# Two graph layers on one core: the first pair of block rows loaded ahead of x, and row scales spread by two DMAs instead of a matrix product

## The chip, the cores and the metric

The kernel runs on one core of one Trainium2 chip. The metric is the device time of one execution in microseconds, lower is better. Every time below comes from three timed runs of the kernel before the change, or from one profiled execution of it.

## The reference

```python
# x: 4096 x 512, adj: 4096 x 4096 (mostly zeros, none negative), W: 512 x 512, all float32
def _L0(cur, inc_m):
    head = (inc_m > 0).astype(float32)
    head = head / maximum(sqrt(sum(head * head, axis=-1)), 1e-12)
    inc = inc_m + head
    return (inc @ cur) / sum(inc, axis=-1)

def _L1(X, A, W):
    A2 = A + eye(4096)
    d = diagonal(A2) ** -0.5
    temp = A2 @ X @ W.T
    return relu((d[:, None] * A2 * d[None, :]) @ temp)

x = layernorm(x + _L0(x, adj))
x = layernorm(x + _L1(x, adj, W))
```

The part that the change touches is `head`: each row of `adj` gets 1/sqrt(number of its positive entries) added to every positive entry. That number per row is counted before the row can be multiplied, and its inverse root is called the row's scale here.

## The kernel before

All large products are float32 and use a Winograd form of Strassen's scheme: seven products of quarter matrices instead of eight, with sums of quarters as operands. The work has two stages.

**First stage (layer 0, and the sums for layer 1).** A *pair* is two blocks of 128 rows of `adj`, rows j and j + 16 in blocks; there are 16 pairs (`NP`). A pair is cut into four *chunks* (`NC`) of four quarters by 512 columns each, 1 MB, laid out by the host in `adj_q` with the row on the free axis (so that the chunk can be the left operand). Chunk n = 4j + c goes through these steps:

- `load_chunk` (L280) on SP's queue into a ring of three tiles `a`.
- `prepare1` (L373), all on VectorE: L383 adds two raw quarters into `sr` (kept for layer 1 and written to DRAM by POOL at L403, into `oa`); L393 makes a mask, (a > 0) times the scale, for one half, and L395 adds it to `a`, for each half; `add_up` (L156 to L162) makes the four sums `s`. `sr` and the two masks are three tiles of one ring of three (`half_tile`, tag `u`).
- `multiply1` (L405): 4 x 7 products on TensorE (L417; each float32 product stands as two records in the profile) into seven PSUM banks that add up over the four chunks.

When a pair is through, `combine` (L419) takes the seven banks out on ScalarE and VectorE, `layer0` (L445) normalises, `operands` (L458) makes the sums of the next stage's right operands and writes them to DRAM (`ob`). The right operands of this first stage are made from x: `load_x` (L285) brings two blocks of x into a slot, and `build` (L295), four VectorE instructions through `outer_sums` (L121), makes four sums in it. There are 16 slots, all kept.

The scales: `count` (L339) lets ScalarE take the sign of tiles of 128 rows by 512 columns of `adj` in natural order (`nat`, five tiles, loaded by SP), with a running sum per row: 16 tiles give a pair's counts, one per row, with the row on the partition axis. `prepare1` wants the scale along the free axis and on all partitions. So `spread` (L351) turns it: a reduction (L355), `to_scale` (L304 to L308, two VectorE instructions and a square root on ScalarE), a reciprocal (L360), a diagonal matrix times the two scales (L363), a product with a matrix of ones on TensorE (L368) into the spare bank, and a copy to `sc` by ScalarE (L370). For the first pair `count_first` (L310) takes the signs of its four chunks and sums them with products by a matrix of ones (L320), which gives the counts on all partitions at once. The fourth chunk is loaded once for this into the tile `last` and again later for its products.

The order is written out by hand: each engine runs its instructions in the order in which the code issues them, and SP's and POOL's queues do likewise. Before the loop SP loads x for slots 0 to 3, three chunks, the fourth chunk, and the rest of x mixed with natural tiles. In the loop, chunk n + 1 is prepared ahead of the products of chunk n, and the first pair's later slots are built in its rounds c = 0, 1, 2. A pair's spread begins at c = 2 of the pair before (c = 3 for the first).

**Second stage (layer 1).** Two passes of products over all of `adj` (`multiply2`, L243, products at L252), the projection by W (L625), and the last normalisation. The change does not touch it.

Of the kernel before, what the change touches and what calls it, by code (L numbers as in the profile page):

```python
# [8 lines left out]
F32 = mybir.dt.float32  # L9
BF16 = mybir.dt.bfloat16  # L10
# [16 lines left out]
def tile_adj_resnorm_d2(  # L27
# [67 lines left out]
    def spare():  # L95
        return bank(7)
# [8 lines left out]
    nc.gpsimd.memset(eps_t, LN_EPS)  # L105
    tiny = const.tile([P, 1], F32, name="tiny")
    nc.gpsimd.memset(tiny, -(2.0 ** -63))
    dscale = const.tile([P, NB], F32, name="dscale")
    nc.gpsimd.dma_start(out=dscale, in_=diag)

# [10 lines left out]
    def outer_sums(t, b11, b12, b21, b22):  # L121

        nc.vector.tensor_sub(t[:, 0, :], b11, b12)
        nc.vector.tensor_sub(t[:, 2, :], b22, b12)
        nc.vector.scalar_tensor_tensor(t[:, 1, :], t[:, 0, :], -1.0, b22, op0=ALU.mult, op1=ALU.subtract)
        nc.vector.tensor_add(t[:, 3, :], b21, t[:, 1, :])

# [139 lines left out]
    w1_pool = scope.enter_context(tc.tile_pool(name="w1", bufs=2))  # L267
    pools["turn"], pools["work"] = [ring] * 2, work

    ones_f = w1_pool.tile([P, P], F32, name="ones_f", bufs=1)  # L270
    nc.gpsimd.memset(ones_f, 1.0)
    ones_b = w1_pool.tile([P, P], BF16, name="ones_b", bufs=1)
    nc.gpsimd.memset(ones_b, 1.0)
    chunks, sums, slots, counts, scale, natural = {}, {}, {}, {}, {}, {}
    xr = {}

    def half_tile(dtype=F32, width=CW):
        return w1_pool.tile([P, 2, width], dtype, tag="u", name="u", bufs=3)

    def load_chunk(n):  # L280
        a = ring.tile([P, 4, CW], F32, tag="a", name="a")
# [2 lines left out]

    def load_x(kk):  # L285

        s = feats_pool.tile([P, 7, W], F32, name=f"b{kk}")
        lo, hi = x[kk * P:(kk + 1) * P, :], x[(kk + NP) * P:(kk + NP + 1) * P, :]
        nc.sync.dma_start(out=s[:, B11:T4 + 1:T4, 0:H], in_=split(lo))
        nc.sync.dma_start(out=s[:, B21:B22 + 1, 0:H], in_=split(hi))  # L290
        nc.gpsimd.memset(s[:, B11:B21 + 1, H:W], 1.0)
        nc.gpsimd.memset(s[:, T1, H:W], 1.0)
        slots[kk] = s

    def build(kk):  # L295

        s = slots[kk]
        outer_sums(s[:, T1:T4 + 1, 0:H], s[:, B11, 0:H], s[:, T4, 0:H], s[:, B21, 0:H], s[:, B22, 0:H])

    def signs(y, a, accum=None):  # L300

        nc.scalar.activation(y, a, AF.Sign, bias=tiny, scale=2.0 ** 64, accum_out=accum)  # L302

    def to_scale(n, total):  # L304

        nc.vector.tensor_scalar(n, total, 0.5, N / 2, op0=ALU.mult, op1=ALU.add)
        nc.vector.tensor_scalar(n, n, EPS * EPS, None, op0=ALU.max)
        nc.scalar.activation(n, n, AF.Sqrt)  # L308

    def count_first(parts):  # L310

        ps = spare()[:, 0:2 * P].rearrange("p (h i) -> p h i", h=2)
        for c, a in enumerate(parts):
            m = half_tile(BF16, 2 * CW)
            m = m.rearrange("p h (q i) -> p (h q) i", q=2)
            signs(m, a)
            for i in range(CK):
                for z in range(2):
                    first, last = c + i + z == 0, c == NC - 1 and i == CK - 1 and z == 1
                    nc.tensor.matmul(ps, ones_b, m[:, z::2, i * P:(i + 1) * P], start=first, stop=last)  # L320
        s = w1_pool.tile([P, 2, P], F32, name="sc")
        to_scale(s, ps)
        nc.vector.reciprocal(s, s)
        scale[0] = s

    tiles = iter([(j, h, t) for j in range(1, NP) for h in range(2) for t in range(NT)])
    waiting = []
# [18 lines left out]
            signs(nat, nat, counts[j][:, h, t:t + 1])  # L346
            load_natural()

    spreading = {}

    def spread(j, part):  # L351

        if part == 0:
            n = small.tile([P, 2], F32, name="n")
            nc.vector.tensor_reduce(n, counts.pop(j), axis=mybir.AxisListType.X, op=ALU.add)  # L355
            to_scale(n, n)
            spreading[j] = n
        elif part == 1:
            n = spreading.pop(j)
            nc.vector.reciprocal(n, n)  # L360
            d = w1_pool.tile([P, 2, P], F32, name="d", bufs=1)
            for h in range(2):
                nc.vector.tensor_scalar(d[:, h, :], ident, n[:, h:h + 1], None, op0=ALU.mult)  # L363
            spreading[j] = d
        else:
            d = spreading.pop(j)
            ps = spare()
            nc.tensor.matmul(ps[:, 0:2 * P], ones_f, d.rearrange("p h i -> p (h i)"), start=True, stop=True)  # L368
            s = w1_pool.tile([P, 2, P], F32, name="sc")
            nc.scalar.copy(s.rearrange("p h i -> p (h i)"), ps[:, 0:2 * P])  # L370
            scale[j] = s

    def prepare1(n, pieces=1):  # L373


        j, c = divmod(n, NC)
        a, s = chunks[n], scale[j]
        sr, *masks = (half_tile() for _ in range(3))
        sums[n] = work.tile([P, 4, CW], F32, tag="s", name="s")
        for i in range(pieces):  # L380
            w = CW // pieces
            cols = slice(i * w, (i + 1) * w)
            nc.vector.tensor_add(sr[:, :, cols], a[:, A11:A22 + 1, cols],  # L383
                                 a[:, A21, cols].unsqueeze(1).to_broadcast([P, 2, w]))
            for h in range(2):
                t = masks[h]
                y, z = t[:, :, cols], a[:, 2 * h:2 * h + 2, cols]
                if pieces == 1:
                    parts = [[v.rearrange("p q (b i) -> p (q b) i", i=P) for v in (y, z)]]
                else:  # L390
                    parts = [[v[:, q, :].rearrange("p (b i) -> p b i", i=P) for v in (y, z)] for q in range(2)]
                for m, v in parts:
                    nc.vector.scalar_tensor_tensor(m, v, 0.0, s[:, h, :].unsqueeze(1).to_broadcast(list(v.shape)),  # L393
                                                   op0=ALU.is_gt, op1=ALU.mult)
                nc.vector.tensor_add(a[:, 2 * h:2 * h + 2, cols], a[:, 2 * h:2 * h + 2, cols], t[:, :, cols])  # L395
            add_up(sums[n][:, :, cols], a[:, :, cols])
# [6 lines left out]
        nc.gpsimd.dma_start(out=dst, in_=sr.rearrange("p m (k i) -> p (m k) i", i=P))  # L403

    def multiply1(n, acc):  # L405
        c = n % NC
# [58 lines left out]
        nc.gpsimd.dma_start(out=in_outer(2, j, slice(T1, T4 + 1)), in_=t)  # L465


    for kk in range(CK):
        load_x(kk)
    for n in range(3):  # L470
        load_chunk(n)
    last = work.tile([P, 4, CW], F32, tag="s", name="s")
    nc.sync.dma_start(out=last, in_=adj_q[0, NC - 1])
    for kk in range(CK, NP):
        load_x(kk)
        if kk >= 2 * CK and len(waiting) < 5:
            load_natural()
    for kk in range(CK):
        build(kk)
    count_first([chunks[0], chunks[1], chunks[2], last])  # L480
    prepare1(0, pieces=CK)

    C = None
    for n in range(NP * NC):
        j, c = divmod(n, NC)
        if c == 0:
            if j > 0:
                C = combine(acc)
            acc = [bank(m) for m in range(7)]
        if n + 2 >= NP * NC:  # L490
            load_up_to(n + 2 - NP * NC)
        elif n > 0:
            load_chunk(n + 2)
        if j == 0 and c < NC - 1:
            for kk in range((c + 1) * CK, (c + 2) * CK):
                build(kk)
        if j + 1 < NP and c == (3 if j == 0 else 2):
            spread(j + 1, 0)
            if j == 0:
                spread(1, 1)  # L500
                spread(1, 2)
        if n + 1 < NP * NC:
            prepare1(n + 1)
        else:
            prepare(0)
        if 0 < j < NP - 1 and c == 2:
            spread(j + 1, 1)
        multiply1(n, acc)
        if 0 < j < NP - 1 and c == 2:
            spread(j + 1, 2)  # L510
        count(((5, 5, 6, 4) if j == 0 else (6, 6, 0, 4))[c])
        if j == 1 and c == 1:
# [300 lines left out]
```

## Time and profile before

| what | value |
|---|---|
| median of three runs | 2345.42 us (2344.67 to 2349.24) |
| profiled execution | 2345.41 us |
| its span, first to last instruction | 2343.6 us |
| mean granted TensorE clock | 0.990 |
| busy: TensorE, VectorE, ScalarE, POOL | 2277.4, 1832.7, 351.5, 220.7 us |
| end of the first stage's products | 834.55 us |

PE is the TensorE row for products and PEld for loading the left operand, which overlaps it. DVE is VectorE, ACT ScalarE, POOL GpSimd, and SP the engine whose queue issues most loads. In rows of the form "line engine operation out<-in", tile names are those of the program without their numbers. In brackets stands how long the engine was idle before the instruction and what ended that; if several things were waited for, only the last by the profile is named. In a row of windows the columns are the stretch, its length, busy time with number of instructions for PE, PEld, DVE, ACT and POOL, the granted TensorE clock, the busy share of the DMA engines, and GB/s.

### The profile page before, as it was taken

The page shows a single profiled execution, that of the slowest core. Times are in us where ns is not written, and L with a number is a line of the kernel's source. Part 1 is how long each engine was busy: PE and PEld are TensorE (multiplying, and loading weights), DVE is VectorE, ACT ScalarE, POOL GpSimd, SP SyncE. Part 2 cuts the span into 40 slices and gives each one's busy share as a digit, 9 for nine tenths or more (in the row PEclk, how much of TensorE's full clock was granted, in tenths as well). Part 3 has the DMA queues.
Part 4 walks back from the last instruction along what each step waited for, and adds up shares of the span by engine and source line. Part 5 has one row for each costly group of instructions (what it writes and reads, how often), then busy time and mean ns, then how long its engine had stood idle before and what let it go on. Part 6 is the DMA issues. An engine that isn't in the chain of part 4 may idle for free.

```text
span 2343.6 us, 21028 instructions
## 1 busy us (share of the span) xinstructions
PE 2277.4 (97%) x7166; PEld 1352.6 (58%) x7166; DVE 1832.7 (78%) x2727; ACT 351.5 (15%) x806; POOL 220.7 (9%) x372
## 2 busy tenths in 40 slices
PE   4999999999999999999999999999999999999996
PEld 3788888888888844444444444444444444444443
DVE  6898888888889857888666779766567798767796
ACT  3232333323333000000000000000000011200013
POOL 0011111111111110000001100011100000000010
PEclk8999999999999999999999999999999999999998
DMA  9577777777776466575566757567666576765672
GB/s 318 197 252 252 262 244 253 258 255 260 251 256 235 172 261 242 207 276 204 202 252 229 274 186 267 186 237 286 225 238 223 214 253 237 267 231 216 224 260 77
DMA packets 148011, 552.97 MB, mean 236 GB/s; under 512 B 15920, under 2 KB 24128, under 8 KB 108864
## 3 DMA queue, kind: packets, MB, share of 16 engines
q1 hardware_dynamic: 114192, 418.42, 51.0%
q0 software_dynamic: 33712, 133.21, 14.9%
q8 instruction: 57, 0.93, 0.2%
q14 instruction: 50, 0.41, 0.0%
HBM read 438.32 MB, written 113.25 MB: 235 GB/s over the span
## 4 chain that ended last, share of the span: by engine, by line
PE 86%; DVE 8%; issue 3%; DMA 2%; ACT 0%; POOL 0%; SPq 0%; ACTq 0%; DVEq 0%; POOLq 0%
PE q L252 55%; PE q L417 26%; PE q L625 5%; DVE a L395 1%; DVE u L393 1%; DVE s L159 1%; DMA a<-oa 1%; DVE u L383 1%; DMA s<-adj_q 1%; DVE s L161 1%; PE q L645 1%; DMA oa<-u 0%; DVE c L553 0%; DVE s L162 0%; PE q L368 0%
## 5 line engine op out<-in xcount | busy, mean ns | idle before, releaser
L252 PE MATMUL q<-s,ts 128*128 128x512 f32 x1344 | 616.0, 594 | 1.0 <-DVE u L544 1.0
L417 PE MATMUL q<-b,s 128*128 128x256 f32 (+1 forms) x2048 | 488.5, 381 | 2.3 <-DVE s L161 2.3
L159 DVE TENSOR_TENSOR s<-a 128x1024 f32<-128x1024 f32 (+1 forms) x243 | 294.1, 1210 | 203.5 <-PE q L252 173.8
L252 PEld LDWEIGHTS q<-s,ts 128*128 128x128 f32 x1344 | 256.2, 191 | 325.7 <-issue 296.6
L417 PEld LDWEIGHTS q<-b,s 128*128 128x128 f32 x2048 | 389.8, 190 | 61.0 <-DVE s L161 3.7
L417 PE MATMUL q<-b,a 128*128 128x258 f32 (+1 forms) x1536 | 381.8, 383 | 10.1 <-issue 10.1
L252 PE MATMUL q<-a,tr 128*128 128x512 f32 x704 | 333.5, 596 | 5.1 <-DMA tr<-ob 4.2
L417 PEld LDWEIGHTS q<-b,a 128*128 128x128 f32 x1536 | 293.9, 192 | 52.9 <-issue 10.7
L252 PE MATMUL q<-s,tr 128*128 128x512 f32 x448 | 228.8, 592 | 0.0
L252 PEld LDWEIGHTS q<-a,tr 128*128 128x128 f32 x704 | 132.1, 191 | 162.1 <-issue 158.1
L302 ACT ACTIVATE nat<-nat,tiny 128x512 f32<-128x512 f32 x240 | 171.0, 715 | 208.2 <-DMA nat<-adj 208.1
L252 PE MATMUL q<-a,ts 128*128 128x512 f32 x352 | 180.2, 593 | 3.1 <-DVE c L549 2.9
L393 DVE SCALAR_TENSOR_TENSOR u<-a,sc 128x1024 f32<-128x1024 f32 (+1 forms) x142 | 157.6, 1114 | 24.8 <-ACT sc L370 14.4
L161 DVE TENSOR_TENSOR s<-a,s 128x512 f32<-128x512 f32 (+1 forms) x243 | 166.5, 685 | 8.3
L162 DVE TENSOR_TENSOR s<-a,s 128x512 f32<-128x512 f32 (+1 forms) x243 | 166.5, 685 | 8.3
L395 DVE TENSOR_TENSOR a<-a,u 128x1024 f32<-128x1024 f32 (+1 forms) x134 | 157.7, 1177 | 6.8
L252 PEld LDWEIGHTS q<-s,tr 128*128 128x128 f32 x448 | 85.1, 190 | 107.3 <-issue 99.0
L542 ACT COPY p<-q 128x512 f32<-128x512 f32 x28 | 16.4, 585 | 754.9 <-PE q L252 754.9
L252 PEld LDWEIGHTS q<-a,ts 128*128 128x128 f32 x352 | 66.5, 190 | 88.7 <-issue 77.0
L625 PE MATMUL q<-wt,c 128*128 128x512 f32 x256 | 115.1, 592 | 0.0
L159 DVE TENSOR_TENSOR s<-r 128x1024 f32<-128x1024 f32 x48 | 58.7, 1223 | 70.1 <-PE q L252 65.0
L403 POOL DMA_DIRECT2D oa<-u x64 | 57.6, 901 | 465.8 <-DVE u L383 211.2
(121 smaller groups left out, 1581.2 us busy)
## 6 DMA issues: line engine op xcount, KB each, us to landing
a<-adj_r SPq DMA_DIRECT2D x112, 1024.0 KB, 6.1
a<-oa SPq DMA_DIRECT2D x80, 1024.0 KB, 5.3
a<-adj_q SPq DMA_DIRECT2D x64, 1024.0 KB, 6.1
nat<-adj SPq DMA_DIRECT2D x240, 256.0 KB, 6.9
tr<-ob SPq DMA_DIRECT2D x112, 512.0 KB, 3.7
oa<-u POOLq DMA_DIRECT2D x64, 512.0 KB, 7.9
oa<-r POOLq DMA_DIRECT2D x32, 1024.0 KB, 6.6
y<-x POOLq DMA_DIRECT2D x64, 256.0 KB, 6.1
```

The source lines that it names most:

```text
L159: nc.vector.tensor_add(s[:, S3:S1 + 1, :], a[:, A11:A22 + 1, :], a[:, A21, :].unsqueeze(1).to_broadcast([P, 2, w]))
L161: nc.vector.tensor_add(s[:, S2, :], a[:, A11, :], s[:, S1, :])
L162: nc.vector.tensor_add(s[:, S4, :], a[:, A12, :], s[:, S2, :])
L252: nc.tensor.matmul(acc[m], left, right, start=(kk == 0), stop=(kk == NQ - 1))
L302: nc.scalar.activation(y, a, AF.Sign, bias=tiny, scale=2.0 ** 64, accum_out=accum)
L383: nc.vector.tensor_add(sr[:, :, cols], a[:, A11:A22 + 1, cols], a[:, A21, cols].unsqueeze(1).to_broadcast([P, 2, w]))
L393: nc.vector.scalar_tensor_tensor(m, v, 0.0, s[:, h, :].unsqueeze(1).to_broadcast(list(v.shape)), op0=ALU.is_gt, op1=ALU.mult)
L395: nc.vector.tensor_add(a[:, 2 * h:2 * h + 2, cols], a[:, 2 * h:2 * h + 2, cols], t[:, :, cols])
L403: nc.gpsimd.dma_start(out=dst, in_=sr.rearrange("p m (k i) -> p (m k) i", i=P))
L417: nc.tensor.matmul(acc[m][:, 0:w], left, b[:, right, 0:w], start=(kk == 0), stop=(kk == NP - 1))
L625: nc.tensor.matmul(pv, C_of[2][h][f][:, 2 * r + e, cols], wt[:, 2 * f + e, :], start=(f + e == 0), stop=(f + e == 2))
L645: nc.tensor.transpose(ps[:, at + i * P:at + (i + 1) * P], C_of[3][h][d // 2][:, 2 * r + d % 2, cols], ident)
```

## The change

Before the loop: SP loads the four chunks first, then x for eight slots, five natural tiles, and the rest of x. `count_first` takes each chunk's signs in two halves as the chunk lands, into slots 12 to 15 of x, which are still empty. The raw sums of chunks 0 and 1 are made and written out early (`raw_sums`, split from `prepare1`). Only slot 0 is built before the scale is ready; then the first 128 columns of chunk 0 are prepared, slot 1 is built, the other 384 columns follow, and then slots 2 and 3. `build` has three instructions instead of four. `to_scale` is a single square root on ScalarE with scale and bias; the clamp follows it as a maximum. A square root of a constant is put at the start of ScalarE's work.

In the loop: a single tile `mask` serves both halves, and `sr` has two tiles of its own. The first pair counts 8, 8, 0, 4 natural tiles in its rounds, and each pair's spread begins at c = 2. The spread is a write of the row scales (128 x 2 values) to DRAM and a read of that row back on all 128 partitions, both on POOL's queue, placed between the raw sum and the masks of the next chunk. The scale lies as (row, half) in its tile, so that a mask reads every second value. `ones_f`, the diagonal, the product L368 and the copy L370 are gone.

```diff
+    half_n = const.tile([P, 1], F32, name="half_n")
+    nc.gpsimd.memset(half_n, N / 2)
+    nc.scalar.activation(small.tile([P, 1], F32, name="sd"), eps_t, AF.Sqrt)
...
     def build(kk):
-        s = slots[kk]
-        outer_sums(s[:, T1:T4 + 1, 0:H], s[:, B11, 0:H], s[:, T4, 0:H], s[:, B21, 0:H], s[:, B22, 0:H])
+        s = slots[kk][:, :, 0:H]
+        nc.vector.tensor_sub(s[:, T1:T3 + 1:2, :], s[:, B11:B22 + 1:2, :],
+                             s[:, T4, :].unsqueeze(1).to_broadcast([P, 2, H]))
+        rest_of_sums(s[:, T1:T4 + 1, :], s[:, B21, :], s[:, B22, :])
...
     def to_scale(n, total):
-        nc.vector.tensor_scalar(n, total, 0.5, N / 2, op0=ALU.mult, op1=ALU.add)
-        nc.vector.tensor_scalar(n, n, EPS * EPS, None, op0=ALU.max)
-        nc.scalar.activation(n, n, AF.Sqrt)
+        nc.scalar.activation(n, total, AF.Sqrt, bias=half_n, scale=0.5)
...
+    def count_first(n, c, a, ps):
+        m = slots[NP - NC + c][:, 0:4, 0:H].bitcast(BF16)
+        for z in range(2):
+            signs(m[:, z::2, :], a[:, z::2, :])
             for i in range(CK):
+                first, last = c + i + z == 0, c == NC - 1 and i == CK - 1 and z == 1
+                nc.tensor.matmul(ps.rearrange("p i h -> p h i"), ones_b, m[:, z::2, i * P:(i + 1) * P], start=first, stop=last)
...
     def spread(j, part):
         if part == 0:
             n = small.tile([P, 2], F32, name="n")
             nc.vector.tensor_reduce(n, counts.pop(j), axis=mybir.AxisListType.X, op=ALU.add)
             to_scale(n, n)
-            spreading[j] = n
+            scale[j] = n
...
+        else:
+            n = scale.pop(j)
+            nc.vector.tensor_scalar(n, n, EPS, None, op0=ALU.max)
+            nc.vector.reciprocal(n, n)
+            row = dram.tile([P, 2], F32, name=f"sc{j}")
+            nc.gpsimd.dma_start(out=row, in_=n)
+            scale[j] = w1_pool.tile([P, P, 2], F32, name="sc")
+            nc.gpsimd.dma_start(out=scale[j].rearrange("p i h -> p (i h)"),
+                                in_=row.rearrange("i h -> (i h)").partition_broadcast(P))
...
+    def raw_sums(n):
         j, c = divmod(n, NC)
+        a, sr = chunks[n], w1_pool.tile([P, 2, CW], F32, name="sr", bufs=2)
+        nc.vector.tensor_add(sr, a[:, A11:A22 + 1, :], a[:, A21, :].unsqueeze(1).to_broadcast([P, 2, CW]))
         if j // CK == c:
             add_identity(sr[:, :, (j % CK) * P:(j % CK + 1) * P])
...
+    def to_inc(n, cols):
+        a, s = chunks[n], scale[n // NC]
+        for h in range(2):
+            y, z = mask[:, :, cols], a[:, 2 * h:2 * h + 2, cols]
...
+            for m, v in parts:
+                nc.vector.scalar_tensor_tensor(m, v, 0.0, s[:, :, h].unsqueeze(1).to_broadcast(list(v.shape)),
+                                               op0=ALU.is_gt, op1=ALU.mult)
+            nc.vector.tensor_add(z, z, y)
+        add_up(sums[n][:, :, cols], a[:, :, cols])
+
+    def prepare1(n, between=None):
+        if n not in early:
+            raw_sums(n)
+        if between is not None:
+            between()
+        sums[n] = work.tile([P, 4, CW], F32, tag="s", name="s")
+        to_inc(n, slice(0, CW))
...
-    for kk in range(CK):
-        load_x(kk)
-    for n in range(3):
+    for n in range(NC - 1):
         load_chunk(n)
     last = work.tile([P, 4, CW], F32, tag="s", name="s")
     nc.sync.dma_start(out=last, in_=adj_q[0, NC - 1])
-    for kk in range(CK, NP):
+    ps = spare()[:, 0:2 * P].rearrange("p (h i) -> p i h", h=2)
+    for c in range(NC):
+        count_first(0, c, chunks[c] if c < NC - 1 else last, ps)
+    for kk in range(2 * CK):
         load_x(kk)
-        if kk >= 2 * CK and len(waiting) < 5:
-            load_natural()
-    for kk in range(CK):
-        build(kk)
-    count_first([chunks[0], chunks[1], chunks[2], last])
-    prepare1(0, pieces=CK)
+    while len(waiting) < 5:
+        load_natural()
+    for kk in range(2 * CK, NP):
+        load_x(kk)
+    for n in range(2):
+        early.add(n)
+        raw_sums(n)
+    build(0)
+    scale[0] = w1_pool.tile([P, P, 2], F32, name="sc")
+    to_scale(scale[0], ps)
+    nc.vector.tensor_scalar(scale[0], scale[0], EPS, None, op0=ALU.max)
+    nc.vector.reciprocal(scale[0], scale[0])
+    sums[0] = work.tile([P, 4, CW], F32, tag="s", name="s")
+    to_inc(0, slice(0, P))
+    build(1)
+    to_inc(0, slice(P, CW))
+    build(2)
+    build(3)
...
-        if j + 1 < NP and c == (3 if j == 0 else 2):
+        scales = j < NP - 1 and c == 2
+        if scales:
             spread(j + 1, 0)
-            if j == 0:
-                spread(1, 1)
-                spread(1, 2)
         if n + 1 < NP * NC:
-            prepare1(n + 1)
+            prepare1(n + 1, between=(lambda: spread(j + 1, 1)) if scales else None)
         else:
             prepare(0)
-        if 0 < j < NP - 1 and c == 2:
-            spread(j + 1, 1)
         multiply1(n, acc)
-        if 0 < j < NP - 1 and c == 2:
-            spread(j + 1, 2)
-        count(((5, 5, 6, 4) if j == 0 else (6, 6, 0, 4))[c])
+        count(((8, 8, 0, 4) if j == 0 else (6, 6, 0, 4))[c])
```

More of the change, by code (lines that the diff above doesn't have):

```diff
@@ L124, in outer_sums, with rest_of_sums @@
         nc.vector.tensor_sub(t[:, 2, :], b22, b12)
+        rest_of_sums(t, b21, b22)
+    def rest_of_sums(t, b21, b22):
         nc.vector.scalar_tensor_tensor(t[:, 1, :], t[:, 0, :], -1.0, b22, op0=ALU.mult, op1=ALU.subtract)
@@ L268, in tile_adj_resnorm_d2 @@
     pools["turn"], pools["work"] = [ring] * 2, work
-    ones_f = w1_pool.tile([P, P], F32, name="ones_f", bufs=1)
-    nc.gpsimd.memset(ones_f, 1.0)
     ones_b = w1_pool.tile([P, P], BF16, name="ones_b", bufs=1)
@@ L275, in tile_adj_resnorm_d2 @@
     xr = {}
-    def half_tile(dtype=F32, width=CW):
-        return w1_pool.tile([P, 2, width], dtype, tag="u", name="u", bufs=3)
+    mask = w1_pool.tile([P, 2, CW], F32, name="mask", bufs=1)
     def load_chunk(n):
@@ L285, in load_x @@
     def load_x(kk):
-        s = feats_pool.tile([P, 7, W], F32, name=f"b{kk}")
+        s = slots[kk]
         lo, hi = x[kk * P:(kk + 1) * P, :], x[(kk + NP) * P:(kk + NP + 1) * P, :]
@@ L292, in load_x @@
         nc.gpsimd.memset(s[:, T1, H:W], 1.0)
-        slots[kk] = s
     def build(kk):
-        s = slots[kk]
-        outer_sums(s[:, T1:T4 + 1, 0:H], s[:, B11, 0:H], s[:, T4, 0:H], s[:, B21, 0:H], s[:, B22, 0:H])
+        s = slots[kk][:, :, 0:H]
+        nc.vector.tensor_sub(s[:, T1:T3 + 1:2, :], s[:, B11:B22 + 1:2, :],
+                             s[:, T4, :].unsqueeze(1).to_broadcast([P, 2, H]))
+        rest_of_sums(s[:, T1:T4 + 1, :], s[:, B21, :], s[:, B22, :])
     def signs(y, a, accum=None):
@@ L304, in to_scale @@
     def to_scale(n, total):
-        nc.vector.tensor_scalar(n, total, 0.5, N / 2, op0=ALU.mult, op1=ALU.add)
-        nc.vector.tensor_scalar(n, n, EPS * EPS, None, op0=ALU.max)
-        nc.scalar.activation(n, n, AF.Sqrt)
[L310 to L316, printed above, removed]
-            for i in range(CK):
[L318 to L324, printed above, removed]
+        nc.scalar.activation(n, total, AF.Sqrt, bias=half_n, scale=0.5)
[3 more added lines that the diff above has]
+            signs(m[:, z::2, :], a[:, z::2, :])
+            for i in range(CK):
+                first, last = c + i + z == 0, c == NC - 1 and i == CK - 1 and z == 1
+                nc.tensor.matmul(ps.rearrange("p i h -> p h i"), ones_b, m[:, z::2, i * P:(i + 1) * P], start=first, stop=last)
     tiles = iter([(j, h, t) for j in range(1, NP) for h in range(2) for t in range(NT)])
@@ L347, in count @@
             load_natural()
-    spreading = {}
     def spread(j, part):
@@ L356, in spread @@
             to_scale(n, n)
-            spreading[j] = n
-        elif part == 1:
-            n = spreading.pop(j)
+            scale[j] = n
+        else:
+            n = scale.pop(j)
+            nc.vector.tensor_scalar(n, n, EPS, None, op0=ALU.max)
             nc.vector.reciprocal(n, n)
[L361 to L371, printed above, removed]
@@ L373, in prepare1 @@
-    def prepare1(n, pieces=1):
-        j, c = divmod(n, NC)
[L377 to L396, printed above, removed]
@@ new lines, in spread @@
+            row = dram.tile([P, 2], F32, name=f"sc{j}")
[3 more added lines that the diff above has]
+                                in_=row.rearrange("i h -> (i h)").partition_broadcast(P))
+    early = set()
+    def raw_sums(n):
+        j, c = divmod(n, NC)
+        a, sr = chunks[n], w1_pool.tile([P, 2, CW], F32, name="sr", bufs=2)
+        nc.vector.tensor_add(sr, a[:, A11:A22 + 1, :], a[:, A21, :].unsqueeze(1).to_broadcast([P, 2, CW]))
@@ L403, in prepare1 @@
         nc.gpsimd.dma_start(out=dst, in_=sr.rearrange("p m (k i) -> p (m k) i", i=P))
+    def to_inc(n, cols):
+        a, s = chunks[n], scale[n // NC]
+        for h in range(2):
+            y, z = mask[:, :, cols], a[:, 2 * h:2 * h + 2, cols]
+            if cols == slice(0, CW):
+                parts = [[v.rearrange("p q (b i) -> p (q b) i", i=P) for v in (y, z)]]
+            else:
+                parts = [[v[:, q, :].rearrange("p (b i) -> p b i", i=P) for v in (y, z)] for q in range(2)]
+            for m, v in parts:
[10 more added lines that the diff above has]
+        to_inc(n, slice(0, CW))
     def multiply1(n, acc):
@@ L465, in operands @@
         nc.gpsimd.dma_start(out=in_outer(2, j, slice(T1, T4 + 1)), in_=t)
-    for kk in range(CK):
-        load_x(kk)
-    for n in range(3):
+    for kk in range(NP):
+        slots[kk] = feats_pool.tile([P, 7, W], F32, name=f"b{kk}")
+    for n in range(NC - 1):
         load_chunk(n)
```

## The prediction

> **What bounds the kernel now.** I read the page first (shares, slices, chain), then the chain in order of time at both ends of the stage that changes, then the timeline and the DMA landings there.
>
> ```profile
> PE 2277.4 (97%) x7166; PEld 1352.6 (58%) x7166; DVE 1832.7 (78%) x2727; ACT 351.5 (15%) x806; POOL 220.7 (9%) x372
> PE   4999999999999999999999999999999999999996
> PE 86%; DVE 8%; issue 3%; DMA 2%; ACT 0%; POOL 0%; SPq 0%; ACTq 0%; DVEq 0%; POOLq 0%
> ```
>
> TensorE is full everywhere but in the first slice (58.6 us) and the last, and carries 86% of the chain. Two things can shorten such a kernel: fewer instructions on TensorE, and an earlier point from which it is full. The chain over the first 120 us (start, length, what):
>
> ```profile
> 8.06 12.58 DMA s<-adj_q
> ...
> 20.75 2.01 ACT u L302
> ...
> 25.11 1.75 DVE sc L323
> 26.86 0.28 DVE u L383
> ...
> 46.82 1.14 DVE u L393
> ...
> 83.53 0.09 DVE n L355
> ...
> 86.24 33.85 PE q L417 x150
> ```
>
> The fourth chunk lands at 20.66, its signs end at 22.75, the scale is ready at 26.86. From there to 86 the chain lies on VectorE, which builds operands and prepares chunks 0 to 3. TensorE is in pieces meanwhile (window, TensorE busy first, clock behind PEclk):
>
> ```profile
> 40.00:50.00 10.00, 4.18 (x19) 3.33 (x18) 9.83 (x20) 3.74 (x10) 1.80 (x2) 0.89 1.02 354
> 80.00:90.00 10.00, 4.98 (x14) 4.11 (x15) 8.77 (x14) 3.40 (x10) 0.00 (x0) 0.66 0.45 147
> ```
>
> After 86 the same chain is TensorE alone, a pair of block rows every 48.96 us: 48.53 of the pair's products, 0.43 of L368, which spreads the next scale (starts 381.58 and 382.01 below):
>
> ```profile
> 333.21 48.53 PE q L417 x224
> 382.17 48.53 PE q L417 x224
> ```
> ```profile
> 381.58 0.59 PE L368 MATMUL q<-d,ones_f 128*128 128x256 f32 x2
> 382.01 1.03 PE L417 MATMUL q<-b,a 128*128 128x258 f32 x4
> ```
>
> VectorE is close behind in this stage. Its waits in the same pair (brackets), and POOL's issues:
>
> ```profile
> 371.11 0.90 POOL L403 DMA_DIRECT2D oa<-u  x1
> 372.00 0.55 POOL L463 DMA_DIRECT2D ob<-z  x1
> 382.61 1.23 DVE L393 SCALAR_TENSOR_TENSOR u<-a,sc 128x1024 f32<-128x1024 f32 x1 [0.97 <-ACT sc L370]
> 392.24 0.42 DVE L427 TENSOR_TENSOR z<-q,p 128x256 f32<-128x256 f32 x1 [1.89 <-DMA y<-x]
> ```
>
> The second wait is really for the pair's last products, since L426 copied the first bank until 392.11; so this is VectorE's spare time ahead of the evacuation.
>
> **The change part by part.** All against the profiled execution: 2345.41 us with a span of 2343.6, equal to the median of the runs, 2345.42.
>
> *Chunks ahead of x.* Now 2.1 MB of x go first and the fourth chunk lands at 20.66. From 10 to 20 us the DMA moved 420 GB/s, so a 1 MB chunk takes 2.5 us; the first x transfer landed 3.1 us after its issue. Four chunks issued from 0.74 then land at about 5.4, 7.9, 10.4 and 13.0.
>
> *Early raw sums.* They fill idle VectorE time (L383 1.14 us each, plus L166 0.34 once), before x is there. But each sends 0.5 MB through POOL while chunks still load, from about 8.6 us on. Such a write took 6.8 to 9.0 us at full DMA load (issues at 40 and 47 us) and 3.4 alone: some 5 us for 0.5 MB, a quarter of the bandwidth. Over the 4.4 us left that makes the fourth chunk about 1.1 us late: 14.1. Against this row stands the Trainium skill, "DMA: Bandwidth & Descriptors", Queues, rings and completion order: each DMA engine goes round-robin over its queues packet by packet. Equal turns would put all 1.05 MB ahead of the chunk: 2.5 us late, and the sum below 1.4 worse. I keep the row and let the range hold the rule.
>
> *Count to scale.* Two signs of 128x1024 (between 0.72 for 512 and 1.99 for 2048: 1.13 each), the last four products 0.55 (eight took 1.03), the square root straight from PSUM 0.45 (L308 0.42), the maximum 0.35, L323 1.75: with gaps 5.35 after the chunk, ready at 19.45 instead of 26.86. The root now reads PSUM with a stride; none such is in the trace: bounds 0.4 and 0.8, once; I take the near row. The early Sqrt hides its table load (1.28) in ScalarE's idle start; before, both loads were covered (the first by the fourth chunk's landing, the second by L320 to L307). Without it 0.75 would show. build(0) now stands ahead of maximum and reciprocal on VectorE, so late x delays the scale and all behind it: x0 lands 1.7 after the chunk (512 KB at three quarters of the rate), and is built 1.5 later, just level with the root. That edit costs nothing, but with no room.
>
> *VectorE from the scale on.* Four builds took 54.32 to 60.18, 5.86; a build of three instructions instead of four is 1.5 (the 128x512 subtraction costs 0.70, two of 128x256 cost 0.67), so 6.0. A chunk without raw sum took 46.82 to 54.32, 7.5. With one mask tile the second mask overwrites what the sum just read: L431 to L432, such a pair, starts no sooner than a dependent one, so 0.1 more, 7.6. In order: first block 2.8 (27.14 to 29.97), build 1.5, other 384 columns 6.1 (three quarters of 7.5 and four more starts), two builds 3.0, four 6.0, chunk 1 7.6, four 6.0, chunk 2 8.7, four 6.0, reduction 0.2, chunk 3 with raw sum and part of the spread 9.1: 57.0. TensorE's last run-up starts 1.5 before that end (the last instruction, 0.7, and two products of a chunk's left quarters, 0.86, lie beside it): 19.45 + 55.5 = 75.0. Before it was 86.04. **Gain 11.0.** TensorE will have finished chunk 2 by then (ready near 60, 12.1 long). Chunk 3 must reload after chunk 0's products (about 34) and, on SP, behind eight natural tiles whose slots ScalarE frees when x 8 to 15 have landed (near 42): it lands near 50 and is wanted at 67. Natural tiles 0 to 15 are counted by 55, wanted at 67. So SP's new order costs nothing.
>
> *Spread without TensorE.* The first spread is in 86.04 already; 14 others of 0.43 leave a full TensorE. **Gain 6.0.** L306, L307, L363 and L370 go as well: VectorE saves some 0.9 a pair against 0.2 for the maximum and 0.4 for the mask; ring waits on the write (0.59 in that pair) go too, as the raw sum has two tiles of its own.
>
> *The new wait.* Behind the raw sum's write (issued 371.11) POOL issues the row at 372.0, waits for it to land, and issues the broadcast. Neither is in the trace; near them are 128 KB of ob issued at the same place, 7.3 us, and 16 KB of dscale in an empty queue, 2.6. The row is tiny but queued behind 0.5 MB, so I take 7.3: 379.3. The DMA moved only 27 GB/s in 379 to 381, so the broadcast (128 KB) gets 2.9: 382.3. VectorE, with what it saves, comes for it at 380.3, waits 2.0, and has 4.6 to give in that pair: 1.89 of spare time, 1.3 until the next pair's first products want the banks, and the savings. TensorE sees nothing. The rule (same page, the fixed cost of a DMA: about 2 us) would have both done by 376.6 and VectorE not waiting at all; the sum is the same, the margin 2 us larger. Behind POOL's wait stand three ob writes (wanted in the next stage), the next raw sum's write (its tile is reused two chunks later), and the rows of x, issued 25 us ahead of use at 95.9 (wanted 121.1): nothing.
>
> *Stride.* L393 reads the scale with every second value. No row has this. Bounds: nothing, or half rate. "SBUF — State Buffer", SBUF cachelines, wants two accesses per 16-byte line; this has two. I take nothing.
>
> Sum: 2345.4 - 11.0 - 6.0 = 2328.4.
>
> **The rivals.**
> 1. *As summed:* 2328.4, own range 2323 to 2333.
> 2. *The scale is late in every pair:* both DMAs take the loaded 7.3, landing at 386.7. From 384.9 on each microsecond is TensorE's: 1.8 in 15 pairs, 27 us, so 2355. From 1.1 us a pair the kernel is slower than before. For it: the next chunk's 1 MB is issued at 381.8, right on the broadcast. Against it: the empty queue before.
> 3. *The DMA takes the head's gain back:* raw sums by equal turns, and x in 1 KB runs later than reckoned, so that build(0) to build(3) hold VectorE. 6 of the 11 us lost: 2334.
> 4. *Strided reading at half rate:* 8.5 us more a pair on VectorE, over 4 beyond its idle time: above 2400.
> 5. *The wait takes what L368 gave,* and the head moves without TensorE gaining: within 0.2%.
>
> **How the numbers follow.** 0.2% is 4.7 us, about what a measurement of this kernel can tell from no change. Chances: first 0.58, third 0.13 (both faster), second 0.19 (0.03 faster, 0.05 level, 0.11 slower), fourth 0.04, fifth 0.06 (0.04 level, 0.02 slower). Faster 0.74, same 0.09, slower 0.17. The range, 2320 to 2344, takes in the third case and a late scale up to 1 us a pair.
>
> **What would show it.** In the changed profile the chain should leave the last chunk's DMA near 14 us, the reciprocal of 128x256 end near 19.5, TensorE be full from about 75, and a pair take 48.53. VectorE's first product with a pair's scale should show a wait of about 2 us for the broadcast; if above 4.6, and TensorE idle at the same place, the second rival holds. L393 above 1.22 us shows the stride; build(0) waiting for x beyond 17 us, the third.

## The result: no gain, a trace of a loss

The changed kernel takes 2350.22 us (median of 22 runs, 2341.32 to 2359.15), the kernel before 2347.7 in the runs beside them: ratio 1.0017, 95% interval 1.0006 to 1.0028. One run of the kernel before took 5832 us and is left out of the ratio. Forecast was a gain of 17 us; measured is a loss of 2.5 us by the medians, of 4 by the ratio. Its profiled execution has a span of 2348.1 us. The page's busy line, TensorE's slices and the chain's shares by engine:

```profile
PE 2278.6 (97%) x7136; PEld 1346.1 (57%) x7136; DVE 1826.3 (78%) x2644; ACT 348.1 (15%) x795; POOL 236.8 (10%) x402
PE   6999999999999999999999999999999999999996
PE 72%; DVE 15%; DMA 8%; issue 4%; POOL 1%; ACT 1%; SPq 0%; DVEq 0%; ACTq 0%; POOLq 0%
```

TensorE's first slice is fuller (6 instead of 4) and 30 records are gone, the two of each of L368's 15 products. But TensorE carries 72% of the chain where it carried 86%, and DMA 8% where it had 2%: something that waits for transfers now recurs through the first stage. The waits over the whole run name it (who waited for what: sum, times, longest):

```profile
POOL sc L360 <- DMA sc<-n: 112.5, 15, 10.1
DVE mask L388 <- DMA sc<-sc: 67.9, 15, 8.0
PE q L413 <- DVE deg L424: 13.6, 8, 3.0
```

One pair at its worst, from the timelines of POOL, SP, VectorE, ScalarE and TensorE:

```profile
165.10 0.90 POOL L376 DMA_DIRECT2D oa<-sr  x1
165.99 0.55 POOL L358 DMA_DIRECT2D sc<-n  x1
175.31 0.54 POOL L360 DMA_DIRECT2D sc<-sc  x1 [8.77 <-DMA sc<-n]
175.33 0.33 SPq L286 DMA_DIRECT2D a<-adj_q  x1
182.32 1.23 DVE L388 SCALAR_TENSOR_TENSOR mask<-a,sc 128x1024 f32<-128x1024 f32 x1 [6.65 <-DMA sc<-sc]
184.87 0.37 ACT L422 COPY p<-q 128x258 f32<-128x258 f32 x1 [17.60 <-PE q L413]
190.73 0.67 PE L413 MATMUL q<-b,a 128*128 128x258 f32 x2 [2.86 <-DVE deg L424]
```

The row of scales is issued at 165.99, has landed by 175.3, and is then broadcast. SP's next 1 MB chunk goes out 0.02 us behind the broadcast, which takes until 182.3. VectorE has stood still for 6.65 us; it then needs 7.8 us for the chunk, until 190.1, although the first bank has been ready since 184.87. It evacuates the banks that late, and TensorE waits for the second one (L424 reads it). The windows after that pause show a second price in the clock column behind PEclk:

```profile
189.00:191.00 2.00, 0.27 (x1) 0.30 (x2) 1.88 (x5) 0.99 (x3) 0.00 (x0) 1.00 0.91 353
191.00:193.00 2.00, 2.00 (x7) 1.64 (x6) 1.78 (x5) 0.30 (x2) 0.00 (x0) 0.64 0.91 310
193.00:195.00 2.00, 2.00 (x6) 1.57 (x5) 2.00 (x4) 0.71 (x2) 0.35 (x1) 0.51 1.05 375
195.00:197.00 2.00, 2.00 (x10) 1.75 (x10) 1.93 (x3) 2.00 (x7) 0.56 (x1) 1.00 0.73 216
```

After the pause TensorE runs at half its clock for 3.4 us (191.54 to 194.95 in the rows of the last section). This pair lost 4.8 us: 2.86 of pause, and the rest with the clock.

**Pair by pair.** L422 starts when a pair's first bank is complete, so the distance of two such starts is a pair's length; on time it is 48.53. The wait stands in brackets at the first L388 of a pair, the loss is the length of the pair that follows the late evacuation, less 48.53:

| wait for the scale, us | 3.2 | 1.6 | 6.7 | 8.0 | 3.9 | 3.5 | 2.4 | 7.1 | 6.1 | 2.8 | 4.8 | 3.1 | 5.8 | 4.1 | 5.0 |
|---|---|---|---|---|---|---|---|---|---|---|---|---|---|---|---|
| pair longer by, us | 2.3 | 0.1 | 4.8 | 2.5 | 0.4 | 0.0 | 0.0 | 4.7 | 1.3 | 0.0 | 0.6 | 0.0 | 1.8 | 0.5 | 1.4 |

Apart from the first, where VectorE still trails from the head, waits up to about 4 us are free or nearly so and longer ones are paid. The losses add to 20.3 us. The balance at the end of the first stage (start of its last L422, 832.05 before and 833.80 after): the head earlier by 11.7 (first such start 97.16, now 85.45), L368's product saved in 14 pairs, 6.0, a small pause of before gone, 0.9, and 20.3 lost: 1.7 later. The second stage, counted from there, took 1514.3 instead of 1511.5; in the eight other kernels below it took 1512.4 to 1514.6, with either head and either spread, so no one part of the change carries it. The single trace of the kernel before is the shortest of the ten, and its execution was 2.3 us below the median of its runs. So this part is probably scatter between executions; one trace does not show it.

### The profile page after: what moved, and what is told of

The parts are those of the page before. It is cut to its first block, busy times and chain, and to the rows that moved or that the text cites. A ratio compares the mean times of both kernels' runs of the same rounds, so it can differ in the third digit from the quotient of the medians.

```text
span 2348.1 us, 20993 instructions
## 1 busy us (share of the span) xinstructions
PE 2278.6 (97%) x7136; PEld 1346.1 (57%) x7136; DVE 1826.3 (78%) x2644; ACT 348.1 (15%) x795; POOL 236.8 (10%) x402
## 4 chain that ended last, share of the span: by engine, by line
PE 72%; DVE 15%; DMA 8%; issue 4%; POOL 1%; ACT 1%; SPq 0%; DVEq 0%; ACTq 0%; POOLq 0%
PE q L259 53%; PE q L413 13%; PE q L630 5%; DMA sc<-n 3%; DVE mask L388 3%; DVE a L390 3%; DVE s L166 2%; DMA sc<-sc 2%; DVE s L168 1%; DMA oa<-sr 1%; DVE sr L369 1%; DMA a<-oa 1%; DMA b<-x 1%; DVE st L148 1%; PE q L650 1%
## 5 line engine op out<-in xcount | busy, mean ns | idle before, releaser
L413 PE MATMUL q<-b,a 128*128 128x258 f32 (+1 forms) x1536 | 381.9, 383 | 21.6 <-DVE deg L424 13.6
L388 DVE SCALAR_TENSOR_TENSOR mask<-a,sc 128x1024 f32<-128x1024 f32 (+2 forms) x134 | 156.9, 1173 | 70.1 <-DMA sc<-sc 67.9
L390 DVE TENSOR_TENSOR a<-a,mask 128x1024 f32<-128x1024 f32 (+2 forms) x130 | 157.1, 1209 | 6.6
L259 PEld LDWEIGHTS q<-a,ts 128*128 128x128 f32 x352 | 66.5, 190 | 89.4 <-issue 76.5
L376 POOL DMA_DIRECT2D oa<-sr x64 | 57.7, 901 | 376.1 <-DVE sr L369 259.8
```

The costliest lines, as they stand in the source:

```text
L259: nc.tensor.matmul(acc[m], left, right, start=(kk == 0), stop=(kk == NQ - 1))
L388: nc.vector.scalar_tensor_tensor(m, v, 0.0, s[:, :, h].unsqueeze(1).to_broadcast(list(v.shape)), op0=ALU.is_gt, op1=ALU.mult)
L390: nc.vector.tensor_add(z, z, y)
L413: nc.tensor.matmul(acc[m][:, 0:w], left, b[:, right, 0:w], start=(kk == 0), stop=(kk == NP - 1))
```

## The experiments

Two theories besides the late scale were open. POOL, which stands still until the row has landed, could hold up the writes queued behind it (*blocked POOL*). Or VectorE itself could have become denser, by the mask overwritten in place and the strided scale (*denser VectorE*). Ratios are to the kernel before on the same chip, with 95% intervals.

### VectorE does not use the broadcast scale

```diff
-            scale[j] = w1_pool.tile([P, P, 2], F32, name="sc")
+            scale[j] = w1_pool.tile([P, P, 2], F32, name="sc" if j > 1 else "sc1", bufs=2 if j > 1 else 1)
...
-        a, s = chunks[n], scale[n // NC]
+        a, s = chunks[n], scale[min(n // NC, 1)]
```

> The changed kernel with all its DMAs, but the masks of pairs 1 to 15 all read the scale of pair 1, so VectorE waits for no later broadcast; POOL still waits for every row to land. The scales of pairs 2 to 15 are therefore not used. Late-scale theory: 17 to 18 us below the kernel before, pairs at 48.53 us. Blocked-POOL theory: no gain, the pairs stay near 50 us. Denser-VectorE theory: no gain either.

Measured 2332.72, ratio 0.9933 (0.9921 to 0.9945), 15.9 us below the kernel before where 17 to 18 were expected. All pairs after the second are 48.53 to 48.59 long; the second still needs its own scale, and lost 1.2. Its waits in the first stage:

```profile
POOL sc L360 <- DMA sc<-n: 121.6, 15, 10.0
DVE mask L388 <- DMA sc<-sc: 3.6, 1, 3.6
```

POOL waits even a little longer for the row than in the changed kernel, and VectorE makes the same instructions at the same durations; only its wait is gone, and with it the loss. Both rival theories fall with this run.

### A longer chain of DMAs

```diff
-            nc.gpsimd.dma_start(out=row, in_=n)
+            first = dram.tile([P, 2], F32, name=f"first{j}")
+            nc.gpsimd.dma_start(out=first, in_=n)
+            nc.gpsimd.dma_start(out=row, in_=first)
```

> The changed kernel with one DMA more in the chain: the row is copied once more in DRAM before it is broadcast, so that each scale comes some 3 to 8 us later. Late-scale theory: past VectorE's spare time each microsecond is TensorE's in each of 15 pairs, so 45 to 120 us above the changed kernel, 2395 to 2470. If the wait were still mostly covered, it would stay below 2370.

Measured 2411.93, ratio 1.0271 (1.0257 to 1.0284).

```profile
DVE mask L390 <- DMA sc<-sc: 130.4, 15, 10.7
PE q L415 <- DVE deg L426: 58.2, 15, 5.1
```

VectorE's wait rose by 62.5 us in all (130.4 from 67.9), the time by some 60 (ratio 1.0271 from 1.0017). Beyond the spare time a microsecond of wait came out as one of the kernel, as the second rival of the prediction has it. That is a sum of two: TensorE's own waits for the banks rose by only 44.6 us (58.2 from 13.6), and the rest goes with the clock, which was halved after ten pauses between pairs instead of two.

### The row ahead of the raw sum's write

```diff
-        if n not in early:
-            raw_sums(n)
         if between is not None:
             between()
+        if n not in early:
+            raw_sums(n)
```

> The changed kernel with the two scale DMAs issued ahead of the raw sum's write instead of behind it. Late-scale theory: the row no longer stands behind 0.5 MB of that write, only behind the normalised rows; it lands some 3 to 4 us earlier, VectorE's waits fall from a median of 4.1 us to 0 to 2, TensorE does not pause: 14 to 17 us below the kernel before. Blocked-POOL theory: POOL now holds the raw sum's write too while it waits, so it is no better than the changed kernel, 2347 to 2355. Denser-VectorE theory: as the changed kernel, 2347 to 2352.

Measured 2330.32, ratio 0.9922 (0.9909 to 0.9936): 18 us below the kernel before, and the fastest median of this study. Every pair is 48.53 to 48.59 long. Waits, and one pair:

```profile
DVE mask L388 <- DMA sc<-sc: 7.9, 8, 3.0
...
POOL sc L360 <- DMA sc<-n: 99.0, 14, 8.5
```
```profile
309.84 1.26 POOL L452 DMA_DIRECT2D x<-z  x2 [11.26 <-ACT z L161]
311.13 0.54 POOL L358 DMA_DIRECT2D sc<-n  x1
318.91 0.54 POOL L360 DMA_DIRECT2D sc<-sc  x1 [7.25 <-DMA sc<-n]
...
322.82 1.23 DVE L388 SCALAR_TENSOR_TENSOR mask<-a,sc 128x1024 f32<-128x1024 f32 x1 [0.48 <-DMA sc<-sc]
```

The gain came, but not for the reason in the expectation. From the row's issue to the broadcast's is 8.1 us (median of 15), exactly as in the changed kernel: the 0.5 MB of the raw sum in front made no difference to the row. What changed is that the row goes out 2.1 us sooner before the end of its pair (20.5 us ahead of L422 here, 18.4 in an undisturbed pair of the changed kernel), and that the broadcast then takes 3.6 us instead of 5.5 (medians, issue to L388 where L388 waited).

The broadcast's time goes with its start on SP's next chunk of 1 MB, which is issued 3.2 us behind it here and 0.8 in the changed kernel (medians of 14 pairs, without the first). Pair by pair, from issue to landing: in the changed kernel the three broadcasts with a chunk within 0.3 us of them took 6.6 to 7.1 us, the six with a start of 1.0 us or more 4.4 to 5.5; here the thirteen with a start of 2.0 to 3.9 took 3.2 to 4.3, and the first, with 0.2, took 6.2. No run moves the chunk alone, and it is not all: with starts of 1.9 and 2.6 us the changed kernel still needed 5.3. What else slows it there stays open.

### Both DMAs on ScalarE's queue

```diff
-            nc.gpsimd.dma_start(out=row, in_=n)
+            nc.scalar.dma_start(out=row, in_=n)
...
-            nc.gpsimd.dma_start(out=scale[j].rearrange("p i h -> p (i h)"),
+            nc.scalar.dma_start(out=scale[j].rearrange("p i h -> p (i h)"),
```

> The changed kernel with both scale DMAs on ScalarE's queue instead of POOL's. Late-scale theory: on a queue of their own they land in some 3 and 5 us, before VectorE wants the scale: 16 to 18 us below the kernel before, unless ScalarE, which now stands still until the row has landed, delays its signs or copies. Blocked-POOL theory: POOL is free, so the same gain. Denser-VectorE theory: no gain, 2347 to 2352.

Measured 2332.42, ratio 0.9930 (0.9917 to 0.9942). The gain is there, the expected 3 us of the row are not:

```profile
407.13 0.33 ACTq L358 DMA_DIRECT2D sc<-n  x1
417.48 0.33 ACTq L360 DMA_DIRECT2D sc<-sc  x1
417.91 0.72 ACT L307 ACTIVATE nat<-nat,tiny 128x512 f32<-128x512 f32 x1 [11.21 <-DMA sc<-n]
```

A row of 1 KB, alone on its queue, needed 10.4 us here (median of 15: 9.0). On the other queues POOL issued 0.5 MB of normalised rows 1 us ahead of it and 0.5 MB of raw sums 0.2 us behind it, and SP a chunk of 1 MB just ahead of it. The early issue again saved the time: VectorE's waits sum to 38.4 us, and only three pairs were longer than 48.6, by 1.1 at most.

### No write of POOL ahead of the row

On top of the kernel with the row first, the normalised rows' writes are moved behind the broadcast:

```diff
-            nc.gpsimd.dma_start(out=x1_rows[j + h * NP], in_=C[h])
+        def write():
+            for h in range(2):
+                nc.gpsimd.dma_start(out=x1_rows[j + h * NP], in_=C[h])
+        return write
...
+            write()
             operands(j - 1, C)
```

> The kernel with the scale DMAs ahead of the raw sum's write, and now the normalised rows' two writes (0.5 MB) also moved behind them, so that no write of POOL is under way when the row goes out. If the row's 7.5 us are due to writes ahead of it, it lands in about 3 us and no wait for the broadcast is left; if they are due to the loads that share the DMA engines, it still takes 6 to 8 us. Time either way within 2 us of the kernel with the row first, since TensorE did not pause there: 2328 to 2332.

Measured 2333.27, ratio 0.9933 (0.9921 to 0.9945), within the noise of the two kernels above.

```profile
POOL sc L360 <- DMA sc<-n: 67.1, 14, 5.7
DVE mask L388 <- DMA sc<-sc: 0.3, 1, 0.3
```

The row now takes 5.7 us from issue to issue (median), 2.4 less: between the two expectations. So the writes under way when it goes out are part of its delay, though not through its own queue's order. The rest probably belongs to the loads: in the first two spreads of this kernel, with 3 and 88 GB/s under way, it is 3.5 to 3.7, in the others, with 171 to 195 GB/s, 4.8 to 6.3. This fits the Trainium skill, "DMA: Bandwidth & Descriptors", Queues, rings and completion order: a DMA's completion lands only after every earlier write of that DMA engine, across its queues (the page says it of SP's and ScalarE's DMAs). The runs show the delay on a separate queue and its fall without the writes; that the completion rather than the data is held up, they do not show.

### Each half alone

The new head with a scale spread by TensorE (in short: the row and its broadcast replaced by the diagonal, L368's product and the copy):

```diff
-            row = dram.tile([P, 2], F32, name=f"sc{j}")
-            nc.gpsimd.dma_start(out=row, in_=n)
...
+            d = w1_pool.tile([P, 2, P], F32, name="d", bufs=1)
...
+        nc.tensor.matmul(ps[:, 0:2 * P], ones_f, d.rearrange("p h i -> p (h i)"), start=True, stop=True)
...
+        nc.scalar.copy(scale[j].rearrange("p i h -> p h i"), ps[:, 0:2 * P].rearrange("p (h i) -> p h i", h=2))
```

> The changed kernel with its new head, single mask tile and early raw sums kept, but each scale spread by a product on TensorE and a copy on ScalarE again. Late-scale theory: the head's 11.7 us stay, L368's 0.43 us a pair come back, no pair waits for a broadcast: 11 to 12 us below the kernel before, ratio 0.995. Blocked-POOL theory: the same, since POOL waits for nothing. Denser-VectorE theory (the mask overwritten in place and the strided scale make VectorE the bound): the pairs still take longer than 48.96 us and the time is within 3 us of the kernel before.

Measured 2341.06, ratio 0.9969 (0.9956 to 0.9981). Pairs are 48.96 again, as expected, but the gain is 7.5 us and not 11 to 12:

```profile
78.22 1.19 PE L368 MATMUL q<-d,ones_f 128*128 128x256 f32 x2 [5.15 <-DVE d L362]
```

Chunk 3's products stand behind the first spread's product, which stands behind VectorE's chunk. The copy that is L422 in the changed kernel starts at 91.25 here. With the row first it starts at 88.94, and there the clock was half for as long ahead of it (6.8 us): so some 2.3 us of the head's 11.7 came from taking that first spread off TensorE. With ScalarE's queue, half clock for 3.4 us, it starts at 87.02, and in the changed kernel, whose clock stayed full, at 85.45: most of these other 3.5 us hang on the clock. My expectation had booked all of it to the loading order.

The old head with the DMA spread for pairs 2 to 15:

```diff
+        elif part == 3:
+            n = spreading.pop(j)
+            nc.vector.reciprocal(n, n)
+            row = dram.tile([P, 2], F32, name=f"sc{j}")
+            nc.gpsimd.dma_start(out=row, in_=n)
+            sc = w1_pool.tile([P, P, 2], F32, name="sc")
...
-            prepare1(n + 1)
+            prepare1(n + 1, between=(lambda: spread(j + 1, 3)) if 0 < j < NP - 1 and c == 2 else None)
```

> The kernel before with its own head, but the scales of pairs 2 to 15 spread by the two DMAs, issued behind the raw sum's write as in the changed kernel (pair 1 keeps its product on TensorE). Late-scale theory: the pairs cost what they cost in the changed kernel, 48.53 plus some 1.4 us each: about 13 us above the kernel before, ratio 1.005 to 1.007. If the loss came from the new head (x landing late, a colder clock), this one gains 6 us instead, 0.9975.

Measured 2367.28, ratio 1.0078 (1.0063 to 1.0092), a loss of 19 us against 13 expected.

```profile
DVE u L405 <- DMA sc<-sc: 64.4, 14, 8.5
DVE u L405 <- DMA oa<-u: 18.4, 7, 5.9
```

The wait for the scale is as in the changed kernel, and the shared ring of three tiles adds waits for the raw sum's write, which also goes out behind POOL's stop. The loss is therefore in the spread, with either head, and the two tiles of its own for `sr` are worth something beside it.

### Raw sums that really go out early

```diff
+    for n in range(2):
+        early.add(n)
+        raw_sums(n)
     for kk in range(2 * CK):
         load_x(kk)
...
-    for n in range(2):
-        early.add(n)
-        raw_sums(n)
     build(0)
```

> The changed kernel with the raw sums of chunks 0 and 1 issued ahead of the last slots' memsets on POOL, so that their 1 MB really goes out while chunks 2 and 3 load (in the changed kernel POOL waited for the count's products and sent it at 17.3 us). The quarter-share estimate: the fourth chunk lands about 1.1 us later than in the changed kernel, its sign starting near 14.5 instead of 13.4. Equal turns of the queues: 2.5 us later, near 16. Nothing at all if the writes start too late.

A single run, 2343.99. In the changed kernel POOL's memsets of slots 12 to 15 waited for the count's products, which read those slots; the writes therefore left at 17.33, after all four chunks. First the changed kernel, then this one:

```profile
13.44 2.19 ACT L307 ACTIVATE b<-s,tiny 128x1024 bf16<-128x1024 f32 x2 [0.34 <-DMA s<-adj_q]
15.01 0.69 DVE L301 TENSOR_TENSOR b<-b 128x512 f32<-128x512 f32 x1 [5.36 <-DMA b<-x]
16.81 0.10 POOL L295 MEMSET b<- 128x4 f32 x1 [2.39 <-PE q L321]
17.33 1.79 POOL L376 DMA_DIRECT2D oa<-sr  x2 [0.38 <-issue]
17.62 1.75 DVE L486 RECIPROCAL sc<-sc 128x256 f32<-128x256 f32 x1
```
```profile
7.83 0.91 POOL L376 DMA_DIRECT2D oa<-sr  x1 [5.42 <-DVE sr L173]
14.89 2.19 ACT L307 ACTIVATE b<-s,tiny 128x1024 bf16<-128x1024 f32 x2 [1.81 <-DMA s<-adj_q]
18.78 0.69 DVE L301 TENSOR_TENSOR b<-b 128x512 f32<-128x512 f32 x1 [9.13 <-DMA b<-x]
20.63 1.75 DVE L486 RECIPROCAL sc<-sc 128x256 f32<-128x256 f32 x1
```

With early writes the fourth chunk is 1.45 us later, between the quarter share (1.1) and equal turns (2.5). But x, behind it, is 3.8 us later, and as build(0) stands ahead of the reciprocal on VectorE, the scale is 3.0 us later. A single time says nothing of the kernel's total.

## Why the prediction was wrong

**Right.** The head: the reciprocal ended at 19.37 (forecast 19.45), VectorE was through with chunk 3 at 77.1 (76.5), the first pair was through 11.7 us earlier (11.0). The first and the last of these were partly luck, as TensorE's products show, before and now:

```profile
22.80 1.03 PE L320 MATMUL q<-u,ones_b 128*128 128x256 bf16 x8 [1.23 <-ACT u L302]
86.04 1.93 PE L417 MATMUL q<-b,a 128*128 128x258 f32 x4
```
```profile
14.64 2.05 PE L321 MATMUL q<-b,ones_b 128*128 128x256 bf16 x8 [0.47 <-ACT b L307]
76.48 2.00 PE L413 MATMUL q<-b,s 128*128 128x256 f32 x8 [2.92 <-DVE s L168]
```

The chunk came at 13.4, not 14.1, since the contention I charged could not occur. The count's products took that back: eight of them need 2.05 us here, and the last four 1.0, where I reckoned 0.55 from a window of full clock; and the terms of the sum alone add to 5.36, so that nothing was left for gaps. (The kernel before shows the same slow products ahead of 20.57, where its first clock record of 1.0 begins; here that record begins at 24.29, and the windows' column says 1.00 ahead of it too.) TensorE's last run-up then began at 76.48, only 9.6 us earlier than before (86.04), not 11.0; the other 2.1 us came from the clock, which was half from 82.01 to 88.84 before and full here.

L368's 6.0 us came as forecast: 48.53 is a pair's length wherever the scale is on time. The strided read costs nothing: L388 takes 1221 ns where L393 took 1220 (means, 128x1024), as forecast. VectorE's spare time, 4.6 us, was about right: the table puts it near 4.

**Wrong.** The step that failed is "the new wait", in two terms of its sum. The row's 7.3 us were 8.1 from issue to issue, with 5.7 to 10.6 between pairs. The broadcast's 2.9 us, taken from an empty queue because the DMA moved only 27 GB/s in 379 to 381, were 5.5, up to 7.1. The second follows in good part from the first, as the pairs above show: the quiet slot ends when SP issues the next chunk, and a row that is late by a microsecond or two sends the broadcast out together with that 1 MB. I read the quiet slot off the profile of before and did not ask how far the broadcast stood from its end. Two smaller errors work against each other: the row goes out 0.9 us later in its pair than reckoned (18.4 us ahead of the first bank's copy, not 19.3), and VectorE comes for the scale 1.8 us later (9.2 ahead, not 11.0; medians, and the forecasts against the copy at 391.74 less L368's 0.43). Together VectorE waits 4.5 us on average (67.9 in 15 pairs) where 2.0 were forecast and about 4 were free. The 2 us for a DMA that the prediction set beside its own terms are further from the 8.1 and 5.5 than those terms.

That average sits on the edge, and that is what a sum with one value per term hides: five of the fifteen pairs cost at most 0.1 us, three 0.4 to 0.6, and seven 1.3 to 4.8. Of the 20.3 us in all, some 3.6 are TensorE's half clock after the pauses of two pairs, which no step had priced. The second rival had the right mechanism and nearly the right place (lateness from 384.9 on in its pair), at a chance of 0.19; it priced 27 us. The bounds for the two unknown DMAs were far apart, and I took the near end for one of them and kept the other for a rival. The range let the scale cost 1 us a pair; 20.3 us in 15 pairs are 1.35.

The wider scatter of the changed kernel (2341 to 2359, before 2345 to 2351 but for one run) fits a time that hangs on when transfers land, but is not shown to come from it: the four kernels whose pairs lose little have four or five runs each, and spread over 4 to 7 us.

**What would have been predicted with the order of one pair of calls changed.** The row ahead of the raw sum's write gains 18.3 us measured, against the 17.0 of the sum, which has no paid wait. The idea of the change is worth its 17 us; where its DMA is issued decides whether they arrive.

## What to carry to other kernels

Where a short chain of DMAs replaces work on a full engine, price it by the slowest landing of its kind in a loaded window and issue it as early as its data are there: here 2 us earlier in the queue decided over some 20 us in the kernel. A quiet slot seen in a profile has an end; say what is issued there, and how late the new transfer may come before it meets it. And where a wait comes close to the cover it has, sum over its spread and not over its middle, since the cover pays only for the part below it.

## What was not expected of the hardware

A DMA of 128 times 8 bytes to DRAM took 2.6 us to its successor's issue in the first spread on ScalarE's queue (69.49 to 72.08) and 3.6 on POOL's with 3 GB/s under way (row first, first spread). On ScalarE's queue, with nothing else in it, it took up to 10.4 us beside 1 MB of POOL's writes and a 1 MB load. Taking all of POOL's writes from in front of it cut it to 5.7; taking only those of the raw sum did nothing (8.1 in both).

The clock records of all ten traces change only on steps of 3.41 us, which lie elsewhere in each trace, and hold 1.0 or 0.5. What halves the clock is not the length of a pause but how much of it falls into one step. Steps of the changed kernel (rows one and two follow each other, and so do three and four), then of the kernel with the row first:

```profile
72.07:75.49 3.42, 1.49 (x7) 0.95 (x5) 3.28 (x3) 0.00 (x0) 0.00 (x0) 1.00 0.95 93
75.49:78.90 3.41, 2.42 (x11) 2.15 (x12) 3.16 (x5) 0.00 (x0) 0.55 (x1) 1.00 0.73 233
188.13:191.54 3.41, 0.81 (x4) 0.76 (x5) 3.14 (x7) 2.16 (x6) 0.00 (x0) 1.00 1.04 381
191.54:194.95 3.41, 3.41 (x10) 2.69 (x9) 3.30 (x7) 0.66 (x2) 0.30 (x1) 0.50 0.98 330
```
```profile
72.73:76.15 3.42, 1.05 (x5) 0.57 (x3) 3.28 (x3) 0.00 (x0) 1.45 (x2) 1.00 0.72 127
76.15:79.56 3.41, 2.47 (x6) 2.02 (x7) 3.31 (x6) 0.00 (x0) 0.00 (x0) 0.50 0.87 295
```

The changed kernel's 2.92 us ahead of chunk 3 are split by a step, 1.93 and 0.99, and the clock stays full. Its 2.86 us at 190.73 have 2.60 in one step, and the next is at half. With the row first, the pause ahead of chunk 3 has 2.36 of its 3.30 us in one step, and half clock follows; with the row alone it is longer, 3.40, but split 1.72 and 1.68, and the clock stays full. Over all ten traces the same holds without exception: a step at full clock with up to 1.93 us without a product was followed by full clock (70 such steps had more than 1 us), one with 1.95 us or more by half clock (71 steps). By this count a pause between 1.95 and 3.9 us costs the clock or not by where it falls among the steps.
